# A two-layer attention kernel with experts: two expert groups per pack, the values' PSUM accumulator as two tiles, and one instruction for the experts' output rows

## The chip, the cores and the metric

The kernel runs on one core of a Trainium2 chip. The metric is the device time of one execution in microseconds, and of several executions the median. The core has a matrix engine (TensorE, PE in the profile, with its weight loads as PEld), three engines for elementwise work (VectorE or DVE, ScalarE or ACT, GpSimd or POOL), and a queue engine (SyncE or SP) that issues most of the transfers. Matrix products accumulate in PSUM; everything else works in SBUF.

## The reference, cut to what matters

There are B = 4 images of 128 channels and 64 x 64 = 4096 positions. Layer 0 is an attention between positions whose queries and keys are two 1x1 convolutions of 64 channels and whose values are a third one of 128. Layer 1 is an attention over the same positions as tokens, and then a layer of 64 experts in which each expert picks the 8 tokens of an image with the highest gate probability.

```python
x = x + conv_attn(_gn(x))                     # score softmax over j: out = einsum('nij,ncj->nci', score, asm)
t = _to_tokens(x)                             # (4, 4096, 128)
t = t + attn(_ln_t(t), Wq, Wk, Wv)
y = _ln_t(t)
probs = softmax(y @ gate_w.T + gate_b, axis=tokens)
topv, topi = top 8 tokens of every expert, of each image
pooled = sum over the 8 tokens of topv * y[topi]         # (4, 64, 128)
h   = gelu(pooled @ weight1[e, :128] + weight1[e, 128])  # 64 experts, 128 -> 512
o   = h @ weight2[e, :512] + weight2[e, 512]             # 512 -> 128
t[topi] += topv * o
return _from_tokens(t)                        # (4, 128, 64, 64)
```

For each expert there are only 4 rows (one for each image) to multiply by two weight matrices of 256 KB each: 32 MB of weights in all for little arithmetic.

## The kernel before

**Attention.** Each image's 4096 query positions are taken in NB = 8 blocks of 512 (BLK). For a block the kernel runs over all 4096 key positions: score products into PSUM (`scores`, L611), exponential by ACT (L620), then the value products, which accumulate over all key positions into one PSUM tile `av` of 128 x 2 x 512 float32, two banks. In layer 0 (`rows_products`, L545) each bank holds the sum of one half of the rows. In layer 1 (`mixed_products`, L573) the products are made with fewer multiplications from sums and differences of quarters, and the two banks hold parts that are combined afterwards. The pool `ps_av` has one buffer, so the next block's first value product must wait until the tile has been read out:

```python
avs[b, layer, n] = ps_av.tile([P, 2, BLK], F32, tag="av", name=f"av{b}_{layer}_{n}")
```

`finish_conv` (L650 to L653) reads it out after a layer 0 block: ACT copies both banks. `finish_attn` (L717 to L726) does so after a layer 1 block: bank 0 goes to `c0` (L723), bank 1 to `c1` (L724), and the two halves of bank 1, exchanged, to `sw` (L725, L726). These four copies are ACT's, but for the last block of images 0 and 1, where `copy` picks DVE for `c0` and `c1`. The very last block (`final`) divides the copies between ACT and DVE (L717 to L720). `finish_attn` goes on with the residual, the second norm and the gate products `pg` (L819 to L836), whose two halves lie in one PSUM tile of one bank; in the last block ACT reads one of the halves and DVE the other.

**Order of the work.** The order of the stages is written by hand: image and layer (0,0), (1,0), (0,1), (2,0), (1,1), (3,0), (2,1), (3,1). `stage` steps generators (the next image's norm and convolutions, routing of the image before, the finishing of the block before) between groups of key positions. Each engine works its instructions in program order; a tile framework adds the semaphore waits and reuses buffers by tag. Waits are per tile: who writes a reused buffer waits for all readers of what was in it.

**Routing.** In the stages of layer 1 and after the last block, the gate scores of an image lie in `M` as 64 experts x 4096 tokens. The eight largest of every expert are found by DVE (L881 finds and replaces them in one row of 4096), and a sum with them as weights gives `pooled`, 128 channels x (64 experts x 4 images). The last image's part is written by `last_route` (L1046), and only after that can the experts begin. `last_scores` then makes the last image's scatter weights in `M`, beside the experts (L881, L1060, L1062).

**Experts.** Sixteen groups of EG = 4 experts. For each group, step by step:

- `first_product` (L1308): one product per expert, `pooled` of 128 x 4 against 128 x 512 of weight 1, into rows 32j to 32j + 3 of one bank of `phs[0]`, a tile which `hidden_sums` (L701) had filled with zeros. DVE copies the bank to `hp` (L1313).
- `hidden`: four PE transposes of 128 x 128 (L1318), into one bank of `pht`; DVE adds the bias of weight 1 to all 512 columns (L1324), of which 16 x 4 belong to real rows and the others to the 28 padding rows of each expert; ACT applies GELU (L1328).
- `second_product` (L1338): 16 products, for each of 4 experts and 4 slices of 128 hidden units, into rows of the PSUM tile `po`. Of the 32 columns that are multiplied, 4 are real.
- every fourth group `by_expert` (L1348 to L1352) copies `po`, transposes it and puts the real rows into `outT`.

The loop runs group g of the first product, group g - 1 of `hidden` and group g - 2 of the second product in one step. The weights were packed earlier to `packed` in DRAM. Eleven places in SBUF hold groups; many are the buffers of tiles of attention that are no longer needed, and each is loaded anew for a later group (`load`, L1201) once its products have been issued.

**The end.** SP issues, in this order, the eight 256 KB reads of `first_pair` (L1379) and four 2 MB reads of `x2` (L1388), the residual, into places 0 to 3 of the weights. Each of two pairs of images then gets the experts' rows: a PE transpose (L1397), `oe` = (rows + bias of weight 2) x `inv_tot` (L1401, L1402, both DVE), products of `oe` with the scatter weights into PSUM (`px`, L1407), sixteen additions by DVE to the residual (L1414, 128 x 1024 each), and sixteen 512 KB writes of the result (L1417).

```python
oe = block_tile("c0", f"oe{i}")[:, :O]
nc.vector.tensor_add(oe, pe[:, :O], w2b)
nc.vector.tensor_scalar(oe, oe, inv_tot[:, i : i + 1], None, op0=ALU.mult)
```

Of the kernel before, what the change touches and what calls it, by code (L numbers as in the profile page):

```python
# [15 lines left out]
P = 128  # L16
# [10 lines left out]
def tile_unshifted(  # L27
# [45 lines left out]

    def sc_tile(name):
        return ps_sc.tile([P, 2, BLK], F32, tag="sc", name=name)

    def ms_tile(name):
        return ps_ms.tile([P, BLK], F32, tag="ms", name=name)
# [448 lines left out]
    def products():  # L527

        if not before:
            return  # L530
        b, layer, n, g, pts = before.pop()
        if g == 0:
            avs[b, layer, n] = ps_av.tile([P, 2, BLK], F32, tag="av", name=f"av{b}_{layer}_{n}")
        (rows_products if layer == 0 else mixed_products)(b, n, g, pts)
        if g == NG - 1:
            after.append(finish(b, layer, n))

    def rows_products(b, n, g, pts):

        for i, pt in enumerate(pts):  # L540
            for h in range(2):
                j = 2 * (2 * g + i) + h
                for r in range(2):
                    rows = bass.ts(r, CR)
                    nc.tensor.matmul(  # L545
                        avs[b, 0, n][:, r, :], lhsT=values[b, 0][rows, j, :], rhs=pt[rows, h, :],
                        start=(j == 0), stop=(j == NJ - 1),
                    )

# [14 lines left out]
    def mixed_products(b, n, g, pts):  # L564

        av = avs[b, 1, n].rearrange("p k (s t) -> p k s t", s=2)
        v, st = values[b, 1], mixed[b]  # L570

        def mm(half, bank, slot, lhsT, rhs, first, final):
            nc.tensor.matmul(  # L573
                av[bass.ts(half, HC), bank, slot, :], lhsT=lhsT, rhs=rhs, start=first, stop=final,
                skip_group_check=True,
            )

        last_g = g == NG - 1
        for i in range(2):
            j = 2 * (2 * g + i)  # L580
            mm(i, 1, 1, v[:, j, :HC], pts[i][0][:, 0, 0, :], g == 0, last_g)
        for i, (p4, tt) in enumerate(pts):
            p = 2 * g + i
            first, final = p == 0, p == NP - 1
            mm(0, 0, 1, v[:, 2 * p + 1, :HC], p4[:, 1, 0, :], first, final)
            mm(1, 1, 0, st[:, p, 0, :], tt[:, 0, :], False, final)
            mm(0, 0, 0, v[:, 2 * p, HC:], p4[:, 1, 1, :], False, final)
            mm(1, 0, 0, st[:, p, 2, :], tt[:, 1, :], first, final)
            mm(0, 1, 0, st[:, p, 1, :], p4[:, 0, 1, :], False, final)
            mm(1, 0, 1, v[:, 2 * p + 1, HC:], tt[:, 2, :], False, final)  # L590
# [54 lines left out]
    def finish_conv(b, n):  # L645
# [4 lines left out]
        nc.scalar.copy(u, av[:, 0, :])  # L650
        nc.scalar.copy(c0, av[:, 1, :])  # L651
# [43 lines left out]

    phs = []

    def hidden_sums():

        phs.append(sc_tile("ph"))  # L700
        nc.scalar.activation(  # L701
            phs[0].rearrange("p k (j c) -> p (k j) c", c=P),
            ident.unsqueeze(1).to_broadcast([P, 2 * BLK // P, P]), AF.Copy, scale=0.0,
        )

    def finish_attn(b, n):
        nm = f"{b}_1_{n}"
# [6 lines left out]
        one, two = slice(0, HB), slice(HB, BLK)  # L714
        if final:

            nc.scalar.copy(c1, av[:, 1, :])  # L717
            nc.vector.tensor_copy(c0, av[:, 0, :])
            nc.scalar.copy(sw[lo, one], av[lo, 1, one])
            nc.vector.tensor_copy(sw[hi, one], av[hi, 0, one])  # L720
        else:
            copy = nc.vector.tensor_copy if n == NB - 1 and b < B // 2 else nc.scalar.copy
            copy(c0, av[:, 0, :])  # L723
            copy(c1, av[:, 1, :])  # L724
            nc.scalar.copy(sw[lo, :], av[hi, 1, :])  # L725
            nc.scalar.copy(sw[hi, :], av[lo, 1, :])  # L726

            nc.vector.tensor_add(c1, c1, sw)
            nc.vector.tensor_add(u[:, two], c1[:, one], c1[:, two])
            nc.vector.tensor_add(u[:, two], u[:, two], c0[:, one])  # L730
            nc.vector.tensor_add(u[:, one], c1[:, two], c0[:, two])
            nc.vector.tensor_add(u[hi, one], u[hi, one], c0[hi, one])
            nc.vector.tensor_add(u[hi, one], u[hi, one], sw[hi, one])
# [82 lines left out]
                M[b // 2] = keep.tile([P, S], F32, tag="M", name=f"M{b // 2}")  # L816
            cand[b] = small.tile([P, NB, 8], F32, tag="cand", name=f"cand{b}")
        hs = slice((b % 2) * E, (b % 2 + 1) * E)
        pg = ms_tile(f"pg{b}_{n}")  # L819
        m = M[b // 2][hs, bass.ts(n, BLK)]  # L820
        for h in range(2):
            part = slice(h * E, (h + 1) * E)
            nc.tensor.matmul(
                pg[part, :HB], lhsT=gate, rhs=tg[:, bass.ts(h, HB)], start=True, stop=True
            )
        for h in range(2):
            part = slice(h * E, (h + 1) * E)
            if final and h == 1:
# [152 lines left out]
    def last_route(b, dst):  # L981
# [64 lines left out]
        nc.vector.tensor_copy(dst[:, :, b], pq[:, :E])  # L1046
        return top, neg

    def last_scores(b, top, neg):
# [231 lines left out]
    for i in range(2):  # L1281
        piece(6, 0, att_tile("sx", 4, f"w6_{i}"), 6)
    piece(6, 1, block_tile("q", "w6_2"), 6)
    mixed_place = seq.tile([P, 6 * BLK], F32, tag="mixed", name="mixed_place", bufs=1)
    piece(10, 0, mixed_place[:, : EG * H], 10)
    piece(9, 0, mixed_place[:, EG * H :], 9)
# [11 lines left out]
    scores = last_scores(B - 1, *last_top)  # L1298
    watch(1)

    pht = ps_av.tile([P, 2, BLK], F32, tag="av", name="pht")
    hps, hTs, pos = {}, {}, {}


    def first_product(g):
        ph = phs[0][:, g % 2, :]
        for j in range(EG):
            nc.tensor.matmul(  # L1308
                ph[j * PAD : j * PAD + B, :], lhsT=pooled[:, g * EG + j, :],
                rhs=weights_at(g, 0, j), start=True, stop=True,  # L1310
            )
        hps[g] = hp = block_tile("c0", f"hp{g}")
        nc.vector.tensor_copy(hp, ph)  # L1313

    def hidden(g):
        pt, hp = pht[:, g % 2, :], hps.pop(g)
        for c in range(NHC):
            nc.tensor.transpose(  # L1318
                pt[:, bass.ts(c, P)], hp.rearrange("p (q c) -> p c q", c=NHC)[:, c, :], ident
            )  # L1320
        hTs[g] = hT = block_tile("c1", f"hT{g}").rearrange(
            "p (c j b) -> p c j b", c=NHC, j=EG
        )
        nc.vector.tensor_tensor(  # L1324
            hT, pt.rearrange("p (c j b) -> p c j b", c=NHC, j=EG),
            w1bT[:, :, bass.ts(g, EG)].unsqueeze(3).to_broadcast([P, NHC, EG, PAD]), op=ALU.add,
        )
        nc.scalar.activation(hT, hT, AF.Gelu)  # L1328

    def second_product(g):  # L1330
        q, k = divmod(g, EG)
        if k == 0:
            pos[q] = ms_tile(f"po{q}").rearrange("p (g o) -> p g o", o=O)
        w2 = [weights_at(g, 1, j).rearrange("p (c o) -> p c o", c=NHC) for j in range(EG)]
        hT = hTs.pop(g)
        for c in range(NHC):
            for j in range(EG):
                nc.tensor.matmul(  # L1338
                    pos[q][bass.ts(j, PAD), k, :], lhsT=hT[:, c, j, :], rhs=w2[j][:, c, :],
                    start=(c == 0), stop=(c == NHC - 1),  # L1340
                )
        if k == EG - 1:
            by_expert(q, pos.pop(q))

    def by_expert(q, po):

# [7 lines left out]
            pt.rearrange("p (k j b) -> p k j b", k=EG, j=EG)[:, :, :, 0:B],  # L1354
        )

    for g in range(E // EG + 2):
        if g < E // EG:
            first_product(g)
        if 0 <= g - 1 < E // EG:  # L1360
            hidden(g - 1)
        if 0 <= g - 2:
            second_product(g - 2)

        for half, now, ahead in ((0, g, 11), (1, g - 2, 10)):
            if 0 <= now and now + ahead < E // EG:
                load(now + ahead, now, half)
        if g == E // EG // 2 + 2:
            next(scores)
            watch(1, phs[0][0:1, 0, 0:1])  # L1370
    next(scores)
# [23 lines left out]
    for i in range(B // 2):  # L1395
# [6 lines left out]
        nc.vector.tensor_scalar(oe, oe, inv_tot[:, i : i + 1], None, op0=ALU.mult)  # L1402
        for n in range(NB):
            px = sc_tile(f"px{i}_{n}")
            for h in range(2):
# [556 lines left out]
```

## Time and profile before

| what | value |
|---|---|
| median of 3 runs | 3240.53 us (3240.45 to 3242.14) |
| the profiled execution's own time | 3240.0 us |
| its span in the trace | 3238.3 us |
| PE busy | 3211.1 us, 99% of the span |
| DVE, ACT, POOL busy | 2152.8, 1278.7, 384.4 us |
| transfers | 222.90 MB, 69 GB/s over the span |
| attention's last value products end | about 3131 us |
| expert loop, first product to last second product | 3150.65 to 3201.86 us |
| first and last `x2` read issued | 3189.42 and 3198.60 us |
| first addition L1414 starts | 3209.09 us |
| last output write issued | 3230.35 us |

The profile is one execution. Its times count from the span's start; the execution's own time is 1.7 us above the span. A group of instructions is shown as line, engine, operation, result <- operands, and after that busy time, mean duration, and the idle time before it with who ended that. "L726" is line 726 of this kernel. In stretches of time, the DMA share is the mean busy share of the core's 16 DMA engines, so 1.0 means that all are busy throughout.

### The profile page before, as it was taken

The numbers are of one execution on the slowest core, as the hardware profiler recorded it, in microseconds if no ns is written. First come the engines' busy times: TensorE is split into PE (matmuls) and PEld (weight loads), VectorE is DVE, ScalarE is ACT, GpSimd is POOL, SyncE is SP. The second block draws the span as 40 slices with busy tenths as digits, with TensorE's granted clock in tenths as the row PEclk, the third lists the DMA queues.
The fourth block names the chain that finished last, engine by engine and source line by source line (L and its number), as shares of the span: only waits on it lengthen the run. The fifth ranks groups of instructions, "written<-read, shape, count | busy, mean of one in ns | idle before, by whom it ended". The sixth has DMA issues, their size and how long they took to land.

```text
span 3238.3 us, 49417 instructions
## 1 busy us (share of the span) xinstructions
PE 3211.1 (99%) x19630; PEld 1573.6 (49%) x19630; DVE 2152.8 (66%) x4320; ACT 1278.7 (39%) x1562; POOL 384.4 (12%) x417
## 2 busy tenths in 40 slices
PE   9999999999999999999999999999999999999997
PEld 5444444444555544444554444444444444446653
DVE  6665577556675668755775667775776566676566
ACT  3344444443433335443333334444333333343342
POOL 0111113210000003240000001332100002010001
PEclk9999999999999999999999999999999999999999
DMA  3221244223232212311120111331231111132159
GB/s 87 52 53 30 75 103 131 74 80 86 72 89 79 69 43 53 72 33 34 46 53 21 40 27 40 81 76 27 42 80 29 31 30 31 24 104 63 28 207 360
DMA packets 369120, 222.90 MB, mean 69 GB/s; under 512 B 275312, under 2 KB 300016, under 8 KB 365168
## 3 DMA queue, kind: packets, MB, share of 16 engines
q1 hardware_dynamic: 364608, 208.51, 24.1%
q10 hardware_dynamic: 3760, 10.10, 0.8%
q8 instruction: 156, 2.56, 0.3%
q0 software_dynamic: 512, 1.05, 0.1%
q14 instruction: 84, 0.69, 0.1%
HBM read 159.75 MB, written 97.19 MB: 79 GB/s over the span
## 4 chain that ended last, share of the span: by engine, by line


## 5 line engine op out<-in xcount | busy, mean ns | idle before, releaser
L620 ACT ACTIVATE pt<-ps 128x1024 f32<-128x1024 f32 x1024 | 1021.7, 1024 | 1461.0 <-PE ps L611 1396.8
L611 PE MATMUL ps<-q,t 128*64 128x512 f32 x4096 | 934.3, 592 | 0.0
L545 PE MATMUL av<-pt,asm 64*128 64x512 f32 x4096 | 922.1, 589 | 1.5 <-ACT sw L726 1.5
L635 DVE TENSOR_TENSOR sacc<-sacc,pt 128x1024 f32<-128x1024 f32 x448 | 586.1, 1308 | 291.6 <-ACT pt L620 267.8
L573 PE MATMUL av<-pt,tt 128*64 128x256 f32 x3072 | 636.2, 379 | 0.0
L545 PEld LDWEIGHTS av<-pt,asm 64*128 64x128 f32 x4096 | 396.0, 187 | 485.8 <-issue 469.3
L559 DVE TENSOR_TENSOR tt<-pt 128x512 f32<-128x512 f32 x512 | 353.9, 692 | 352.5 <-ACT pt L620 335.9
L611 PEld LDWEIGHTS ps<-q,t 128*64 128x64 f32 x4096 | 305.0, 137 | 482.5 <-issue 452.1
L573 PE MATMUL av<-tt,mixed 128*64 128x256 f32 x2048 | 525.6, 379 | 0.0
L573 PEld LDWEIGHTS av<-pt,tt 128*64 128x64 f32 x3072 | 355.9, 137 | 270.2 <-issue 135.0
L611 PE MATMUL ps<-e,e 64*128 64x512 f32 x2048 | 486.1, 592 | 0.0
L611 PEld LDWEIGHTS ps<-e,e 64*128 64x128 f32 x2048 | 196.1, 187 | 235.8 <-issue 232.2
L573 PE MATMUL av<-tt,tt 128*64 128x256 f32 x1024 | 304.6, 379 | 0.0
L573 PE MATMUL av<-pt,mixed 128*64 128x256 f32 x1024 | 304.6, 379 | 0.0
L573 PEld LDWEIGHTS av<-tt,mixed 128*64 128x64 f32 x2048 | 280.5, 137 | 9.2 <-DVE tt L559 0.2
L186 POOL TENSOR_TENSOR l_y<-l_v,mhalf 128x4 f32<-128x4 f32 x64 | 64.9, 1013 | 1634.8 <-DVE l_v L185 1634.5
L560 DVE TENSOR_TENSOR pt<-tt,pt 128x256 f32<-128x256 f32 x512 | 219.6, 429 | 16.2
L561 DVE TENSOR_TENSOR tt<-pt 128x256 f32<-128x256 f32 x512 | 219.5, 429 | 16.4
L573 PEld LDWEIGHTS av<-pt,mixed 128*64 128x64 f32 x1024 | 140.2, 137 | 65.4 <-DVE pt L560 0.3
L573 PEld LDWEIGHTS av<-tt,tt 128*64 128x64 f32 x1024 | 140.1, 137 | 4.8 <-DVE tt L561 0.3
L652 POOL TENSOR_TENSOR u<-u,c 128x512 f32<-128x512 f32 x32 | 40.9, 1277 | 557.5 <-ACT c L651 557.5
L632 DVE TENSOR_TENSOR sacc<-pt,pt 128x1024 f32<-128x1024 f32 x32 | 39.1, 1221 | 50.6 <-ACT pt L620 50.5
(298 smaller groups left out, 1797.6 us busy)
## 6 DMA issues: line engine op xcount, KB each, us to landing
wp<-in_weight_dram SPq DMA_DIRECT2D x128, 256.0 KB, 4.5
w<-wp SPq DMA_DIRECT2D x10, 1024.0 KB, 11.1
w<-wp SPq DMA_DIRECT2D x17, 512.0 KB, 10.7
xq<-in_x_dram SPq DMA_DIRECT2D x32, 256.0 KB, 3.8
rb<-inv SPq DMA_DIRECT2D x32, 256.0 KB, 3.4
xT<-xt SPq DMA_DIRECT2D x128, 64.0 KB, 2.2
ak<-xT SPq DMA_DIRECT2D x32, 256.0 KB, 3.7
t<-kt SPq DMA_DIRECT2D x128, 64.0 KB, 2.2
```

What stands on the lines that cost most here:

```text
L186: nc.gpsimd.tensor_tensor(y[:, :k], v[:, :k], mhalf[:, :k], op=ALU.pow)
L545: nc.tensor.matmul(avs[b, 0, n][:, r, :], lhsT=values[b, 0][rows, j, :], rhs=pt[rows, h, :], start=(j == 0), stop=(j == NJ - 1),)
L559: nc.vector.tensor_sub(tt[:, 0:2, :], p4[:, :, 1, :], p4[:, 0, :, :])
L560: nc.vector.tensor_add(p4[:, 0, 1, :], tt[:, 1, :], p4[:, 0, 0, :])
L561: nc.vector.tensor_sub(tt[:, 2, :], p4[:, 1, 0, :], p4[:, 0, 1, :])
L573: nc.tensor.matmul(av[bass.ts(half, HC), bank, slot, :], lhsT=lhsT, rhs=rhs, start=first, stop=final, skip_group_check=True,)
L611: nc.tensor.matmul(ps[part, h, :], lhsT=key[:, part], rhs=q[rows, :], start=True, stop=True,)
L620: nc.scalar.activation(pt, ps, AF.Exp, scale=scale)
L632: nc.vector.tensor_add(sums[b, n], pts[0], pts[1])
L635: nc.vector.tensor_add(sums[b, n], sums[b, n], pt)
L652: nc.gpsimd.tensor_add(u, u, c0)
```

## The change

There are five edits.

1. `av` becomes two tiles of one bank each (`av_tiles`). At the last block of images 0 and 1 only `c0` stays with DVE; `c1` goes to ACT like the two `sw` copies.
2. In the last block the gate products `pg` go into two PSUM tiles, one for each half.
3. Two groups of experts make a pack (PK = 2). `pooledP` is a copy of `pooled` with 8 columns per expert for each of the two groups: group k of the pack has its 4 rows in columns 4k to 4k + 3, and zeros in the other four. The two groups' first products accumulate in the same bank, 8 rows per expert, so that one copy `hp` and four transposes serve both. The bias of weight 1 is added to the 64 real columns of each slice alone, once per group, which also packs them densely; one GELU of 128 columns serves both groups, and the second product multiplies 4 columns. `hidden` is one tile, of which one half serves even packs and the other odd packs.
4. The tiles `po` are two fixed ones, zeroed once by ACT (`zeros_into`), since the second products no longer write the padding rows. `outT` moves into `pooled`'s place, and the reloads of places follow the packs.
5. The product of the bias of weight 2 with `inv_tot` is made ahead of the loop (`biases`), and `oe` comes from PSUM by one SCALAR_TENSOR_TENSOR.

```diff
+    def av_tiles(name):
+        return [ps_av.tile([P, BLK], F32, tag=f"av{k}", name=f"av{k}_{name}") for k in range(2)]
...
-            avs[b, layer, n] = ps_av.tile([P, 2, BLK], F32, tag="av", name=f"av{b}_{layer}_{n}")
+            avs[b, layer, n] = av_tiles(f"{b}_{layer}_{n}")
...
             copy = nc.vector.tensor_copy if n == NB - 1 and b < B // 2 else nc.scalar.copy
-            copy(c0, av[:, 0, :])
-            copy(c1, av[:, 1, :])
-            nc.scalar.copy(sw[lo, :], av[hi, 1, :])
-            nc.scalar.copy(sw[hi, :], av[lo, 1, :])
+            copy(c0, av[0])
+            nc.scalar.copy(c1, av[1])
+            nc.scalar.copy(sw[lo, :], av[1][hi, :])
+            nc.scalar.copy(sw[hi, :], av[1][lo, :])
...
-        pg = ms_tile(f"pg{b}_{n}")
+        pgs = [ms_tile(f"pg{b}_{n}_{h}") for h in range(2 if final else 1)]
...
+    PK = 2
+    pooledP = block_tile("tb", "pooledP").rearrange("p (e m) -> p e m", e=E)
...
+    nc.gpsimd.memset(pooledP, 0.0)
+    for k in range(PK):
+        nc.gpsimd.tensor_copy(
+            by_pack[0][:, :, k, :, k * B : k * B + B - 1], by_pack[1][:, :, k, :, 0 : B - 1]
+        )
...
-    last_top = last_route(B - 1, pooled)
-    outT = block_tile("tb", "outT")[:, : B * E].rearrange("p (b e) -> p b e", e=E)
+
+    def last_pooled(pq):
+        by = pq.rearrange("p (g k j) -> p g k j", k=PK, j=EG)
+        for k in range(PK):
+            nc.vector.tensor_copy(by_pack[0][:, :, k, :, k * B + B - 1], by[:, :, k, :])
+
+    last_top = last_route(B - 1, last_pooled)
+    outT = pooled.rearrange("p e b -> p (e b)").rearrange("p (b e) -> p b e", e=E)
...
+    phts = av_tiles("pht")
+    pos = [ms_tile(f"po{i}").rearrange("p (g o) -> p g o", o=O) for i in range(2)]
+    for po in pos:
+        zeros_into(po)
+    hidden_place = block_tile("c1", "hidden")
+    biases = [hidden_place[:, BLK // 2 + i * O :][:, :O] for i in range(B // 2)]
+    for i, bias in enumerate(biases):
+        nc.vector.tensor_scalar(bias, w2b, inv_tot[:, i : i + 1], None, op0=ALU.mult)
...
     def first_product(g):
-        ph = phs[0][:, g % 2, :]
+        k, pk = g % PK, g // PK
+        ph = phs[0][:, pk % 2, :]
         for j in range(EG):
             nc.tensor.matmul(
-                ph[j * PAD : j * PAD + B, :], lhsT=pooled[:, g * EG + j, :],
-                rhs=weights_at(g, 0, j), start=True, stop=True,
-            )
-        hps[g] = hp = block_tile("c0", f"hp{g}")
-        nc.vector.tensor_copy(hp, ph)
+                ph[j * PAD : j * PAD + PK * B, :], lhsT=pooledP[:, g * EG + j, :],
+                rhs=weights_at(g, 0, j), start=(k == 0), stop=(k == PK - 1),
+            )
+        if k == PK - 1:
+            hps[pk] = hp = block_tile("c0", f"hp{pk}")
+            nc.vector.tensor_copy(hp, ph)
...
-        nc.vector.tensor_tensor(
-            hT, pt.rearrange("p (c j b) -> p c j b", c=NHC, j=EG),
-            w1bT[:, :, bass.ts(g, EG)].unsqueeze(3).to_broadcast([P, NHC, EG, PAD]), op=ALU.add,
-        )
-        nc.scalar.activation(hT, hT, AF.Gelu)
+        at = hidden_place[:, bass.ts(pk % 2, PK * NHC * EG * B)]
+        hT = at.rearrange("p (k c j b) -> p k c j b", k=PK, c=NHC, j=EG)
...
+        for k in range(PK):
+            g = pk * PK + k
+            nc.vector.tensor_tensor(
+                hT[:, k], p4[:, :, :, bass.ts(k, B)],
+                w1bT[:, :, bass.ts(g, EG)].unsqueeze(3).to_broadcast([P, NHC, EG, B]),
+                op=ALU.add,
+            )
+            hTs[g] = hT[:, k]
+        nc.scalar.activation(at, at, AF.Gelu)
...
-                    pos[q][bass.ts(j, PAD), k, :], lhsT=hT[:, c, j, :], rhs=w2[j][:, c, :],
+                    po[j * PAD : j * PAD + B, k, :], lhsT=hT[:, c, j, :], rhs=w2[j][:, c, :],
...
+    packs = E // EG // PK
+    for pk in range(packs + 1):
+        mine = range(pk * PK, pk * PK + PK) if pk < packs else ()
+        for g in mine:
             first_product(g)
+            reload(g, 11, 0)
+            if g == mine[0] and pk > 0:
+                hidden(pk - 1)
+        if pk == packs:
+            hidden(pk - 1)
+        if pk > 0:
+            for g in range((pk - 1) * PK, pk * PK):
+                second_product(g)
+                reload(g, 10, 1)
+        if pk == packs // 2:
             next(scores)
             watch(1, phs[0][0:1, 0, 0:1])
...
-        nc.vector.tensor_add(oe, pe[:, :O], w2b)
-        nc.vector.tensor_scalar(oe, oe, inv_tot[:, i : i + 1], None, op0=ALU.mult)
+        nc.vector.scalar_tensor_tensor(
+            oe, in0=pe[:, :O], scalar=inv_tot[:, i : i + 1], in1=biases[i], op0=ALU.mult,
+            op1=ALU.add,
+        )
```

More of the change, by code (lines that the diff above doesn't have):

```diff
@@ L545, in rows_products @@
                     nc.tensor.matmul(
-                        avs[b, 0, n][:, r, :], lhsT=values[b, 0][rows, j, :], rhs=pt[rows, h, :],
+                        avs[b, 0, n][r], lhsT=values[b, 0][rows, j, :], rhs=pt[rows, h, :],
                         start=(j == 0), stop=(j == NJ - 1),
@@ L564, in mixed_products @@
     def mixed_products(b, n, g, pts):
-        av = avs[b, 1, n].rearrange("p k (s t) -> p k s t", s=2)
+        av = [t.rearrange("p (s t) -> p s t", s=2) for t in avs[b, 1, n]]
         v, st = values[b, 1], mixed[b]
@@ L573, in mm @@
             nc.tensor.matmul(
-                av[bass.ts(half, HC), bank, slot, :], lhsT=lhsT, rhs=rhs, start=first, stop=final,
+                av[bank][bass.ts(half, HC), slot, :], lhsT=lhsT, rhs=rhs, start=first, stop=final,
                 skip_group_check=True,
@@ L649, in finish_conv @@
         s2 = sums.pop((b, n))
-        nc.scalar.copy(u, av[:, 0, :])
-        nc.scalar.copy(c0, av[:, 1, :])
+        nc.scalar.copy(u, av[0])
+        nc.scalar.copy(c0, av[1])
         nc.gpsimd.tensor_add(u, u, c0)
@@ L696, in tile_unshifted, with zeros_into @@
     phs = []
+    def zeros_into(t):
+        nc.scalar.activation(
+            t, ident.unsqueeze(1).to_broadcast([P, t.shape[1], P]), AF.Copy, scale=0.0
+        )
     def hidden_sums():
         phs.append(sc_tile("ph"))
-        nc.scalar.activation(
-            phs[0].rearrange("p k (j c) -> p (k j) c", c=P),
-            ident.unsqueeze(1).to_broadcast([P, 2 * BLK // P, P]), AF.Copy, scale=0.0,
-        )
+        zeros_into(phs[0].rearrange("p k (j c) -> p (k j) c", c=P))
     def finish_attn(b, n):
@@ L715, in finish_attn @@
         if final:
[L717 to L720, printed above, removed]
+            nc.scalar.copy(c1, av[1])
+            nc.vector.tensor_copy(c0, av[0])
+            nc.scalar.copy(sw[lo, one], av[1][lo, one])
+            nc.vector.tensor_copy(sw[hi, one], av[0][hi, one])
         else:
             copy = nc.vector.tensor_copy if n == NB - 1 and b < B // 2 else nc.scalar.copy
[L723 to L726, printed above, removed]
+            copy(c0, av[0])
+            nc.scalar.copy(c1, av[1])
+            nc.scalar.copy(sw[lo, :], av[1][hi, :])
+            nc.scalar.copy(sw[hi, :], av[1][lo, :])
             nc.vector.tensor_add(c1, c1, sw)
@@ L823, in finish_attn @@
             nc.tensor.matmul(
-                pg[part, :HB], lhsT=gate, rhs=tg[:, bass.ts(h, HB)], start=True, stop=True
+                pgs[-h][part, :HB], lhsT=gate, rhs=tg[:, bass.ts(h, HB)], start=True, stop=True
             )
@@ L827, in finish_attn @@
             part = slice(h * E, (h + 1) * E)
+            pg = pgs[-h]
             if final and h == 1:
@@ L1045, in last_route @@
         nc.tensor.matmul(pq[:, :E], lhsT=halves, rhs=twin, start=False, stop=True)
-        nc.vector.tensor_copy(dst[:, :, b], pq[:, :E])
+        dst(pq[:, :E])
         return top, neg
@@ L1283, in tile_unshifted @@
     piece(6, 1, block_tile("q", "w6_2"), 6)
+    PK = 2
+    pooledP = block_tile("tb", "pooledP").rearrange("p (e m) -> p e m", e=E)
+    by_pack = [
+        t.rearrange("p (g k j) m -> p g k j m", k=PK, j=EG) for t in (pooledP, pooled)
+    ]
+    nc.gpsimd.memset(pooledP, 0.0)
[3 more added lines that the diff above has]
+        )
     mixed_place = seq.tile([P, 6 * BLK], F32, tag="mixed", name="mixed_place", bufs=1)
@@ L1299, in tile_unshifted, with hidden @@
     watch(1)
-    pht = ps_av.tile([P, 2, BLK], F32, tag="av", name="pht")
-    hps, hTs, pos = {}, {}, {}
+    phts = av_tiles("pht")
[3 more added lines that the diff above has]
+    hidden_place = block_tile("c1", "hidden")
+    hps, hTs = {}, {}
+    biases = [hidden_place[:, BLK // 2 + i * O :][:, :O] for i in range(B // 2)]
+    for i, bias in enumerate(biases):
+        nc.vector.tensor_scalar(bias, w2b, inv_tot[:, i : i + 1], None, op0=ALU.mult)
     def first_product(g):
-        ph = phs[0][:, g % 2, :]
+        k, pk = g % PK, g // PK
+        ph = phs[0][:, pk % 2, :]
         for j in range(EG):
             nc.tensor.matmul(
-                ph[j * PAD : j * PAD + B, :], lhsT=pooled[:, g * EG + j, :],
-                rhs=weights_at(g, 0, j), start=True, stop=True,
-            )
-        hps[g] = hp = block_tile("c0", f"hp{g}")
-        nc.vector.tensor_copy(hp, ph)
-    def hidden(g):
-        pt, hp = pht[:, g % 2, :], hps.pop(g)
+                ph[j * PAD : j * PAD + PK * B, :], lhsT=pooledP[:, g * EG + j, :],
+                rhs=weights_at(g, 0, j), start=(k == 0), stop=(k == PK - 1),
+            )
+        if k == PK - 1:
+            hps[pk] = hp = block_tile("c0", f"hp{pk}")
+            nc.vector.tensor_copy(hp, ph)
+    def hidden(pk):
+        pt, hp = phts[pk % 2], hps.pop(pk)
         for c in range(NHC):
@@ L1320, in hidden @@
             )
-        hTs[g] = hT = block_tile("c1", f"hT{g}").rearrange(
-            "p (c j b) -> p c j b", c=NHC, j=EG
-        )
-        nc.vector.tensor_tensor(
-            hT, pt.rearrange("p (c j b) -> p c j b", c=NHC, j=EG),
-            w1bT[:, :, bass.ts(g, EG)].unsqueeze(3).to_broadcast([P, NHC, EG, PAD]), op=ALU.add,
-        )
-        nc.scalar.activation(hT, hT, AF.Gelu)
+        at = hidden_place[:, bass.ts(pk % 2, PK * NHC * EG * B)]
+        hT = at.rearrange("p (k c j b) -> p k c j b", k=PK, c=NHC, j=EG)
+        p4 = pt.rearrange("p (c j m) -> p c j m", c=NHC, j=EG)
+        for k in range(PK):
[7 more added lines that the diff above has]
+        nc.scalar.activation(at, at, AF.Gelu)
     def second_product(g):
         q, k = divmod(g, EG)
-        if k == 0:
-            pos[q] = ms_tile(f"po{q}").rearrange("p (g o) -> p g o", o=O)
+        po = pos[q % 2]
         w2 = [weights_at(g, 1, j).rearrange("p (c o) -> p c o", c=NHC) for j in range(EG)]
@@ L1342, in second_product @@
         if k == EG - 1:
-            by_expert(q, pos.pop(q))
+            by_expert(q, po)
     def by_expert(q, po):
@@ L1355, in by_expert, with reload @@
         )
-    for g in range(E // EG + 2):
-        if g < E // EG:
-            first_product(g)
[L1360 to L1368, printed above, removed]
+    def reload(g, ahead, half):
+        if g + ahead < E // EG:
+            load(g + ahead, g, half)
+    packs = E // EG // PK
+    for pk in range(packs + 1):
+        mine = range(pk * PK, pk * PK + PK) if pk < packs else ()
+        for g in mine:
+            first_product(g)
+            reload(g, 11, 0)
[8 more added lines that the diff above has]
+        if pk == packs // 2:
             next(scores)
```

## The prediction

> **What bounds the kernel now.** I read the page first, then the transfer shares by stretch, then the timeline of single stretches, then the waits. The page says where the bulk is:
>
> ```profile
> PE 3211.1 (99%) x19630; PEld 1573.6 (49%) x19630; DVE 2152.8 (66%) x4320; ACT 1278.7 (39%) x1562; POOL 384.4 (12%) x417
> DMA  3221244223232212311120111331231111132159
> ```
>
> PE is busy for 99%, so up to the last attention block (it ends near 3131 us) only PE time counts, and only what makes PE wait can be won. The DMA row ends in 5 and 9: in the last 160 us the transfers are a second candidate. The same row by stretch of the end (columns: window, its length, busy us of PE, PEld, DVE, ACT, POOL, granted clock, DMA share, GB/s):
>
> ```profile
> 3130.00:3186.00 56.00, 51.31 (x620) 33.59 (x616) 34.21 (x87) 13.19 (x23) 1.05 (x1) 1.00 1.02 408
> 3186.00:3191.00 5.00, 4.37 (x64) 2.40 (x68) 3.35 (x5) 1.26 (x2) 0.00 (x0) 1.00 0.42 134
> 3191.00:3210.00 19.00, 14.57 (x206) 8.23 (x198) 12.02 (x15) 11.77 (x13) 5.65 (x3) 0.90 1.00 415
> 3210.00:3213.00 3.00, 3.00 (x8) 1.09 (x8) 2.04 (x3) 0.44 (x1) 3.00 (x2) 0.51 0.42 173
> 3216.00:3234.00 18.00, 11.35 (x42) 3.01 (x40) 13.14 (x12) 0.00 (x0) 0.00 (x0) 0.98 1.01 398
> ```
>
> From 3130 on the transfers are the bound: a share of 1.0 at 400 to 415 GB/s, with two holes. The first (3186 to 3191) lies between the last expert weights with the `first_pair` reads and the four 2 MB `x2` reads (L1388). The second (3210 to 3213, and a third of 3215 to 3216) lies between those reads and the output writes (L1417). Who makes the holes is in the timeline (start us, us, engine, line, operation; in brackets the idle time before and who ended it):
>
> ```profile
> 3160.30 1.04 PE L1308 MATMUL ph<-w,pooled 128*4 128x512 f32 x8
> 3161.27 0.75 PE L1318 MATMUL pht<-ident,hp 128*128 128x128 f32 x4
> 3161.95 1.08 PE L1338 MATMUL po<-w,hT 128*32 128x128 f32 x32
> 3162.84 1.04 PE L1308 MATMUL ph<-w,pooled 128*4 128x512 f32 x8
> 3186.63 1.04 PE L1308 MATMUL ph<-tt,pooled 128*4 128x512 f32 x8 [2.58 <-DVE hp L1313]
> 3189.42 0.37 SPq L1388 DMA_DIRECT2D t<-x  x1
> 3204.46 4.71 DVE L1402 TENSOR_SCALAR oe<-oe,inv_tot 128x128 f32<-128x128 f32 x2
> 3209.09 1.21 DVE L1414 TENSOR_TENSOR t<-t,px 128x1024 f32<-128x1024 f32 x1
> ```
>
> An expert group costs PE 2.54 us (0.97 first products, 0.68 transposes, 0.89 second products, no gap). The `x2` read at 3189.42 goes into the buffer that groups 10 and 11 used; in SP's waits L1388 waits 12.1 us in all for `po` of L1338. So hole one is the expert loop being late. Hole two is the final additions being late: DVE starts them at 3209.09, after two multiplications of `oe` that took 4.71 us, where the same form at L900 took 0.29. One more place, in the attention part, at a change of batch:
>
> ```profile
> 1158.95 0.69 DVE L723 COPY c<-av 128x512 f32<-128x512 f32 x1 [0.79 <-PE av L573]
> 1159.56 0.68 DVE L724 COPY c<-av 128x512 f32<-128x512 f32 x1
> 1160.33 0.58 ACT L725 COPY sw<-av 64x512 f32<-64x512 f32 x1 [3.42 <-DVE c L724]
> 1160.92 0.58 ACT L726 COPY sw<-av 64x512 f32<-64x512 f32 x1
> 1161.55 3.70 PE L545 MATMUL av<-pt,asm 64*128 64x512 f32 x16 [0.76 <-ACT sw L726]
> ```
>
> Four copies empty the one `av` tile one after the other, ACT behind DVE, and PE waits 0.76 us for the last. The same stands at 1939.19, again 0.76; these two make up the 1.5 us of idle time that the page puts down at L545 to L726; its other large groups of PE matmuls show none.
>
> **What the Trainium skill says.** "PSUM — Partial Sum Buffer", section "PSUM bank collisions raise a hardware error": two engines must not touch one bank at once, two readers included; different banks may be used together. The trace orders even more: at 3131.78 ACT copies one bank of `av`, and DVE's copy of the other bank starts at 3132.40, when ACT's has ended. So the tile is what is ordered, and two tiles should free both. "SBUF — State Buffer", section "Who interferes with whom": DVE's two-port modes, into which `tensor_scalar` can go, share a port pair with GpSimd under an exclusive lock, while a DVE instruction with one SBUF input outside those modes doesn't contend. The trace agrees: L1402 takes 2.4 us each beside POOL's L1062 (2.42 us each, from 3204.35), and L1414 with one PSUM input stays at 1.22 beside it. "DMA: Bandwidth & Descriptors", Specifications, has a fabric ceiling of 435 GB/s; the trace's best stretches, 408 to 415 GB/s at a full share, leave little above.
>
> **The change, part by part.**
> 1. *`av` as two tiles; the second copy at the two batch ends goes from DVE to ACT.* ACT now copies bank 1 (0.59) and the two `sw` halves (0.58 each) from 1158.95 on, done near 1160.73; DVE's bank 0 is done at 1159.64. PE asks for bank 0 at 1160.79. Both stalls go: **2 x 0.76 = -1.52 us**. What is queued behind on ACT, the exponentials of 1161.52, starts 0.8 earlier, although ACT has one copy more. PE is the limit there, so all of it arrives at the end of attention, and every weight load that waits for it moves along.
> 2. *Last block: copies in parallel, `pg` in two tiles.* DVE's `M` add at 3142.50 waited for ACT's 0.47 us; now it doesn't. With the copies some 0.5 to 0.7 us of this chain; the filler products until 3147.74 let through about 0.5. The transfers are full beside it: 0 at the end.
> 3. *Two groups per pack.* First products stay 16 x 0.85: 592 ns per matmul stands for 4 columns (L1308) and for 64 (L611), so 8 cost the same. Transposes: 8 x 0.68 instead of 16 x 0.68, -5.4. Second products with 4 columns instead of 32: the nearest row is the old one, 0.89; bounds 0 and -0.1 per group. Copies `hp` on DVE: 8 x 0.69 instead of 16; bias additions 16 of 64 elements, 0.22 to 0.27 each by the 128x64 copy (L1352, 0.27), for 16 x 0.69; ACT 8 activations of about 0.31 for 16 x 0.63. Waits: the first products of pack 1 wait for the copy of pack 0, and so do those of pack 2 for pack 1 (1.0 us each, as 0.81 at 3152.50 shows for two halves of `ph`); after that the copy hides behind two second products (1.78). The 4.42 us MATCH_REPLACE8 (L881) still stalls PE for about 2.1 (2.58 now). Adding PE's list up from the start of the experts, the loop takes some 42.5 us instead of 51.2 (3150.65 to 3201.86), and group 10's second products end near 3181.7 in the changed run's time (3189.36 now).
> 4. *Added:* a POOL memset and two copies for `pooledP` (a few us near 3122, POOL idle there until 3137); DVE's two bias multiplications (0.29 each, behind the products' latency); two ACT zeroings of `po` (0.6 each, between 3148 and 3150, while ACT waits for the first `hT`); one more small DVE copy ahead of the first product (0.15). Cover: transfers run at full share through all of it. Were it gone, about 0.3 us.
> 5. *`oe` as one SCALAR_TENSOR_TENSOR from PSUM.* 0.35 us by the same form at L763, for 0.5 + 4.71. With 3, the first addition starts near 3196 instead of 3209.09.
>
> What 3 and 5 bring at the end isn't their sum. `x2` reads issued by 3184 close hole one; additions 13 us earlier close hole two. In bytes: hole one 5 x (1 - 134/415) = 3.4 us, with the slow restart 3.8; hole two 3 x (1 - 173/400) = 1.7, and 0.36 at 3215. Together **-5.5 to -5.9**. The sixteen additions (16 x 1.22 = 19.5) end near 3219, long before the last write: DVE has 7 us to spare. After the holes are closed the next to be late is the transfer itself.
>
> Sum: -1.5 - 5.7 = -7.2 on the profiled execution's 3240.0 us (span 3238.3, 1.7 around it) gives 3232.8; the median of the runs is 0.5 above it, so **3233.3**.
>
> **Rivals.**
> - *Both holes close (the forecast).* 3231.5 to 3235.0. For it: full shares on both sides of each hole. Chance 0.62.
> - *A hole stays*, because reads and writes at once move less, or because the loads' buffers come free in pairs: -1.5 and only 2.1 of the rest, 3236.9. Against: the 256 KB write of L780, issued at 3137.76 beside the weight loads, left the total at 395 to 420 GB/s from 3141 to 3144. Chance 0.22. If the two stalls of 0.76 also stay, since something else ends them, 1.5 more.
> - *PE and DVE set the end after all:* 8.7 and 4.4 us arrive, 3226. Against: the 56 us at a share of 1.02. Chance 0.08.
> - *Slower:* a pack runs as one serial chain. `hidden` is a single tile for both halves and the biases, and the trace shows tiles ordered as a whole. Then PE stands for copy 0.97, transposes 0.75, additions 0.5, activation 0.31, hand-overs 0.35: 2.9 us per pack, six packs ahead of group 10: 3199 instead of 3181.7, and the `x2` reads are 9.5 us later than now: 3240 + 9.5 - 2.1 = 3247. It starts to cost at 0.5 us per pack, and turns the result slower above 2.6. Against: PE's order has each transpose behind the second products of the pack before, so the tile is free by then. Chance 0.08.
>
> **Numbers.** 3233.3 us; range 3230.0 to 3237.0: the forecast's own, the open hole, and the edge towards the third case. A change under 0.2% (6.5 us) can't be told from none. Faster by more: most of the first case and the third, 0.62; within it: the second and the rest of the first, 0.31; slower 0.07.
>
> **What would show it.** PE without a gap at L545's successor; a DMA share of 1.0 from 3130 through the last write, no hole over 1 us; first `x2` issue near 3184 and first addition near 3196; `oe` in 0.35 us; transposes 32. Wrong if a hole stays with the loop faster, if PE waits over 0.5 us per pack, or if the GB/s drop where reads and writes mix.

## The result, and the profile after

The changed kernel takes **3232.71 us** (median of 10 executions, 3232.03 to 3233.59); the kernel before, beside it on the same chip, 3241.69 (3240.0 to 3244.1). The ratio is 0.9972 with a 95% interval of 0.9962 to 0.9982, which is 5.8 to 12.3 us less. The two profiled executions took 3240.0 and 3232.45 us, with spans of 3238.3 and 3230.6: 7.6 and 7.7 us less, where the forecast's sum was 7.2. The medians differ by more, 9.0: the profiled execution of the kernel before is the fastest of its ten.

From the page of the changed kernel, the rows that answer to those of before; the last number of the matmul row is the idle time ahead of it:

```profile
PE 3202.3 (99%) x19598; PEld 1574.2 (49%) x19598; DVE 2134.0 (66%) x4311; ACT 1272.0 (39%) x1558; POOL 387.5 (12%) x420
DMA  3121235223232212311221111231131111122149
L548 PE MATMUL av<-pt,asm 64*128 64x512 f32 x4096 | 922.4, 590 | 0.0
```

PE has 32 instructions fewer (the transposes) and 8.8 us less to do, and the value products of L548 (L545 before) have no idle time ahead of them, where 1.5 us stood. From the start of the first exponential of attention to that of the last the trace of before has 3101.15 us (24.56 to 3125.71) and this one 3099.41 (24.41 to 3123.82): 1.74 less, about 0.83 of it at each of the two batch ends. What stands there now, at the first of them:

```profile
1158.75 0.58 ACT L728 COPY c<-av 128x512 f32<-128x512 f32 x1 [2.00 <-PE av L576]
1158.79 0.69 DVE L727 COPY c<-av 128x512 f32<-128x512 f32 x1 [0.79 <-PE av L576]
1159.35 0.58 ACT L729 COPY sw<-av 64x512 f32<-64x512 f32 x1
1159.94 0.58 ACT L730 COPY sw<-av 64x512 f32<-64x512 f32 x1
1160.47 3.80 PE L548 MATMUL av<-pt,asm 64*128 64x512 f32 x16
```

DVE and ACT start within 0.04 us of each other, and PE's L548 has no bracket: it doesn't wait, where L545 waited 0.76 us in the kernel before.

The end of the kernel by stretch (window, length, busy us of PE, PEld, DVE, ACT, POOL, granted clock, DMA share, GB/s):

```profile
3128.00:3148.00 20.00, 18.96 (x152) 16.14 (x148) 12.47 (x54) 6.09 (x13) 1.05 (x1) 1.00 1.02 412
3148.00:3153.00 5.00, 4.10 (x36) 1.17 (x36) 2.26 (x12) 1.93 (x3) 0.00 (x0) 1.00 0.99 332
3153.00:3183.00 30.00, 26.98 (x498) 15.18 (x494) 12.40 (x23) 1.81 (x6) 0.00 (x0) 1.00 1.02 413
3183.00:3187.00 4.00, 4.00 (x36) 1.39 (x25) 1.32 (x4) 0.01 (x1) 0.00 (x0) 1.00 1.08 403
3187.00:3208.00 21.00, 17.51 (x180) 7.95 (x178) 12.38 (x16) 10.29 (x11) 9.44 (x4) 0.92 1.01 419
3208.00:3225.00 17.00, 7.71 (x28) 1.91 (x26) 9.41 (x8) 0.00 (x0) 0.00 (x0) 0.84 1.03 416
```

Both holes are gone: where 134 GB/s (3186 to 3191) and 173 GB/s (3210 to 3213) stood, the share is 1.0 through the reads, the stretch where reads and writes mix, and the writes. One shallow dip has come up, 332 GB/s at 3148 to 3153: 5 x (413 - 332) is 0.4 MB, or 1.0 us of transfers. It will matter below. A pack in the timeline, and the start of the final additions:

```profile
3167.02 1.04 PE L1336 MATMUL ph<-w,pooledP 128*8 128x512 f32 x8
3167.99 0.75 PE L1347 MATMUL av_pht<-ident,hp 128*128 128x128 f32 x4
3168.84 0.35 DVE L1355 TENSOR_TENSOR hidden<-av_pht,w1bT 128x64 f32<-128x64 f32 x2 [2.78 <-PE av_pht L1347]
3169.31 0.31 ACT L1361 ACTIVATE hidden<-hidden 128x128 f32<-128x128 f32 x1 [4.10 <-DVE hidden L1355]
3169.68 1.93 PE L1370 MATMUL po<-w,hidden 128*4 128x128 f32 x64
3195.03 0.61 DVE L1440 SCALAR_TENSOR_TENSOR oe<-poe,inv_tot,hidden 128x128 f32<-128x128 f32 x2 [0.42 <-PE poe L1436]
3197.51 1.22 DVE L1455 TENSOR_TENSOR t<-t,px 128x1024 f32<-128x1024 f32 x1 [1.87 <-PE px L1448]
```

Two groups share one set of transposes and one activation of 0.31 us; PE fills the 0.9 us between its transposes and its second products with the next first products. The two `oe` take 0.61 us together instead of 0.5 + 4.71, and the first addition starts at 3197.51 instead of 3209.09.

### The profile page after: what moved, and what is told of

It reads as the page before. It is cut to its first block, busy times and chain, and to the rows that moved or that the text cites. A ratio compares the mean times of both kernels' runs of the same rounds, so it can differ in the third digit from the quotient of the medians.

```text
span 3230.6 us, 49325 instructions
## 1 busy us (share of the span) xinstructions
PE 3202.3 (99%) x19598; PEld 1574.2 (49%) x19598; DVE 2134.0 (66%) x4311; ACT 1272.0 (39%) x1558; POOL 387.5 (12%) x420
## 3 DMA queue, kind: packets, MB, share of 16 engines
q8 instruction: 156, 2.56, 0.3%
## 4 chain that ended last, share of the span: by engine, by line
PE 98%; DVE 1%; issue 1%; DMA 0%; POOL 0%; SPq 0%; ACT 0%; POOLq 0%; ACTq 0%; DVEq 0%
PE ps L614 41%; PE av L548 27%; PE av L576 24%; PE pq L517 1%; PE pv L759 1%; PE pe L372 1%; PE ph L1336 0%; PE pa L374 0%; PE pa L351 0%; PE pe L319 0%; PE pg L827 0%; PE po L1370 0%; PE px L1448 0%; DVE w L1455 0%; DMA first_x<-in_x_dram 0%
## 5 line engine op out<-in xcount | busy, mean ns | idle before, releaser
L548 PE MATMUL av<-pt,asm 64*128 64x512 f32 x4096 | 922.4, 590 | 0.0
L548 PEld LDWEIGHTS av<-pt,asm 64*128 64x128 f32 x4096 | 401.6, 187 | 478.5 <-issue 477.2
```

Of the source, the lines that this page charges most:

```text
L548: nc.tensor.matmul(avs[b, 0, n][r], lhsT=values[b, 0][rows, j, :], rhs=pt[rows, h, :], start=(j == 0), stop=(j == NJ - 1),)
```

## The experiments

Theory A is the forecast's: from 3128 on the transfers set the end. Theory B, its third rival: PE and DVE do. Where a number stands "against the changed kernel", its median of 3232.71 above and of 3232.26 in the run below is the base. The changed kernel wasn't run again beside the later ones; the kernel before was, with medians of 3241.27 to 3241.69, so the bases carry over to within some 0.5 us, and differences under about 1 us are not told from none.

**The changed kernel again (r1_after).** 

> The changed kernel again, as the base for the other kernels of this row. Both theories: 3232 to 3234 us, 7 to 9 us below the kernel before.

 Measured: 3232.26 us beside 3241.27 for the kernel before.

**`oe` by two instructions again (r2_no_oe).**

```diff
-        nc.vector.scalar_tensor_tensor(oe, in0=pe[:, :O], ...
+        nc.vector.tensor_add(oe, pe[:, :O], w2b)
+        nc.vector.tensor_scalar(oe, oe, inv_tot[:, i : i + 1], None, op0=ALU.mult)
```

> The changed kernel, with oe made again by two instructions (add, then tensor_scalar). The two tensor_scalars fall beside POOL's subtractions and take about 2.4 us each, so the first addition starts about 4.6 us later, near 3202 instead of 3197.5. Theory A (the transfers set the end): the x2 reads keep the transfers busy until 3209, and the first writes can be issued near 3205, so hole two stays closed: 0 to +0.5 us against the changed kernel. Theory B (the chain of PE and DVE sets the end): +4.6 us.

 Measured: 3231.84 us, -0.4 to -0.9 against the changed kernel. In its timeline of DVE, `oe` is slow again beside POOL:

```profile
3195.04 0.49 DVE L1440 TENSOR_TENSOR oe<-poe,w2b 128x128 f32<-128x128 f32 x2 [0.42 <-PE poe L1436]
3195.45 3.87 DVE L1441 TENSOR_SCALAR oe<-oe,inv_tot 128x128 f32<-128x128 f32 x2
3199.24 2.34 DVE L1453 TENSOR_TENSOR t<-t,px 128x1024 f32<-128x1024 f32 x2
```

The first addition is 1.7 us later (4.6 were expected) and the last write is issued 2.8 us later (3220.81 for 3217.96), and the end doesn't move. So DVE's chain does not set it, and in the changed kernel the fifth edit is worth nothing.

**Only `av` in two tiles, with the `c1` copy on ACT (r5_av).** The edit to the kernel before is the first of the change. 

> The kernel before with only av as two tiles and the c1 copy of two batch ends on ACT. Expected: both stalls of 0.76 us gone, the last value products 1.5 to 1.9 us earlier, both holes as before: -1.5 to -1.9 us. Rival: other work takes PE's place or the stalls move to another wait, 0.

 Measured: 3239.12 us, -2.2, ratio 0.9993 (0.9985 to 1.0002): by the interval alone not told from no change, but the trace has attention 1.75 us shorter.

**The two halves of that edit (r6_split, r7_move).**

```diff
r6_split: two tiles, but
-            nc.scalar.copy(c1, av[1])
+            copy(c1, av[1])
r7_move: one tile, but
-            copy(c1, av[:, 1, :])
+            nc.scalar.copy(c1, av[:, 1, :])
```

Each ran once, at 3239.3 and 3242.3 us; what counts is the two stalls in the trace.

> The kernel before with av as two tiles, but c0 and c1 both copied by DVE at the two batch ends. Bank 0 is free 0.7 us after PE's last product; bank 1 waits for DVE's second copy and ACT's two, as before. Expected: each stall stays at 0.6 to 0.8 us, now at the first product into bank 1. Rival (the split alone frees PE): no gap.

 Missed: PE has no gap there, and attention is 1.48 us shorter. The timeline of r6_split:

```profile
1159.43 0.69 DVE L727 COPY c<-av 128x512 f32<-128x512 f32 x1 [0.74 <-PE av L576]
1160.04 0.68 DVE L726 COPY c<-av 128x512 f32<-128x512 f32 x1
1160.16 0.58 ACT L728 COPY sw<-av 64x512 f32<-64x512 f32 x1 [2.73 <-DVE c L727]
1161.15 3.92 PE L548 MATMUL av<-pt,asm 64*128 64x512 f32 x16
```

The order had turned as well: DVE copies bank 1 first (L727), and ACT's copies of bank 1 run beside DVE's copy of bank 0. 

> The kernel before with one av tile, but the c1 copy at the two batch ends on ACT. If a tile is what is ordered, ACT's copies wait for DVE's copy of the other bank: 0.69 + 0.58 + 0.58 + 0.58 instead of 0.69 + 0.68 + 0.58 + 0.58, and each stall is 0.6 to 0.7 us. If only the bank is ordered, ACT and DVE go side by side and the stalls are gone.

 Measured: each stall 0.70, and attention is 0.11 us shorter. The timeline of r7_move:

```profile
1158.78 0.69 DVE L723 COPY c<-av 128x512 f32<-128x512 f32 x1 [0.79 <-PE av L573]
1159.50 0.59 ACT L724 COPY c<-av 128x512 f32<-128x512 f32 x1 [2.77 <-DVE c L723]
1161.33 3.70 PE L545 MATMUL av<-pt,asm 64*128 64x512 f32 x16 [0.70 <-ACT sw L726]
```

ACT's copy of bank 1 starts when DVE's copy of bank 0 has ended: with one tile the tile is ordered, not the bank. So the split brings the gain, in r6_split with the order that came with it, and the move alone 2 x 0.06 us.

**`av` and `oe`, but no packs (r4_av_oe).** The first and fifth edits on the kernel before. 

> The kernel before with av in two tiles (and the c1 copy on ACT) and oe by one instruction, but the expert groups one by one as before. Theory A: hole one stays (the loop is as late as before), hole two closes: about -1.9 for av and -2.4 for hole two, -4.3 us against the kernel before. Theory B: -1.9 and the 4.6 us that oe gets shorter, -6.5.

 Measured: 3237.16 us, -4.1, ratio 0.9987 (0.9981 to 0.9994): theory A's number. By stretch:

```profile
3128.00:3183.00 55.00, 51.74 (x626) 33.87 (x622) 33.38 (x87) 13.08 (x23) 1.04 (x1) 1.00 1.02 410
3184.00:3189.00 5.00, 4.05 (x47) 2.27 (x50) 2.94 (x6) 1.26 (x2) 0.00 (x0) 0.66 0.38 135
3209.00:3211.00 2.00, 1.82 (x8) 0.60 (x8) 1.90 (x3) 1.24 (x2) 2.00 (x1) 1.00 0.99 356
```

Hole one stays; hole two is all but closed (356 GB/s). Hole one isn't quite that of before, though: the second line has a granted clock of 0.66, where the kernel before has 1.00 in its hole. After the stall beside the replacement the clock fell to 0.5 from 3185.3 to 3188.8, so that PE freed the place of the first `x2` read late:

```profile
3184.95 1.52 PE L1315 MATMUL ph<-tt,pooled 128*4 128x512 f32 x8 [2.58 <-DVE hp L1320]
3189.24 0.37 SPq L1395 DMA_DIRECT2D t<-x  x1
```

The read goes out 4.3 us after the end of the stall, for 2.8 in the kernel before (3186.63 and 3189.42). Over 8 us around the hole this kernel moves 145 GB/s (3184 to 3192), the kernel before 220 (3185 to 3193): at 410 GB/s that is 5.2 us lost, for 3.7. r5_av has the same drop of the clock (157 GB/s in 3184 to 3192).

With the packs in its place, r2_no_oe has both holes closed. Against r5_av the `oe` edit alone brings -2.0, the packs alone (r2_no_oe) -7.3, and both -6.4 to -6.9: the packs close both holes, and `oe` only the second.

**`pg` in one tile again (r8_no_pg).** 

> The changed kernel, with pg of the last block in one tile again. DVE's M addition waits for ACT's read, about 0.5 us on the chain to the experts' start. Theory A (transfers set the end): 0 against the changed kernel. Theory B: up to +0.5.

 Measured: 3232.74 us, 0 to +0.5. Its M addition waits again for ACT (1.24 us idle ahead of it, 0.74 in the changed kernel), and the end doesn't show it. Little of it gets as far as the experts: from attention's last value product to the first expert product it takes 18.83 us (3128.14 to 3146.97), for 18.66 in the changed kernel (3129.43 to 3148.09). Between the gate products and the routing's next PE work stand 50 filler products (5.85 us) in both.

**1.5 MB of weights loaded earlier (r3_early).**

```diff
+            for i, first in ((0, NG // 2), (1, NG // 2 + 1)):
+                if first <= g < first + EG - 1:
+                    load_piece(i, 1, pieces[i, 1][g - first])
...
-                load(0, 0, 1)
+                load_piece(0, 1, pieces[0, 1][EG - 1])
-    load(1, 1, 1)
+    load_piece(1, 1, pieces[1, 1][EG - 1])
```

> The changed kernel, with second-half weights of groups 0 and 1 loaded in pieces of one expert (256 KB): three of four pieces each are issued during the last attention block, as soon as the quarter of the keys or values that they overwrite has been used, instead of at the block's end. So 1.5 MB leave the stretch that is full of transfers for one in which the DMA share is 0.35. Theory A: 1.5 MB at 410 GB/s are 3.8 us; about 0.7 us of it lost again in a hole ahead of the first x2 read, whose place PE frees at 3182.4: -3.0 us against the changed kernel. Theory B: 0, since no instruction of PE or DVE is touched and no weight was waited for.

 Missed: 3233.79 us, 1.1 to 1.5 **more** than the changed kernel. Theory A can't be right as it stands, so two kernels asked where a megabyte counts.

**One megabyte less early, or moved early with few pieces (r9_less_first, r11_early2).** The first leaves out `load(1, 1, 1)`, and group 1's second products use what is in the place. The second:

```diff
+            for i, first in ((0, NG // 2), (1, NG // 2 + 1)):
+                if first <= g < first + 2:
+                    part_of_second(i, g - first, 1)
...
-                load(0, 0, 1)
+                part_of_second(0, 2, 2)
-    load(1, 1, 1)
+    part_of_second(1, 2, 2)
```

> The changed kernel without one 1 MB weight load (second half of group 1), which is issued at the end of attention and lands near 3140; group 1's second products read what was in the place, so part of the result is not the reference's. Theory A as I had it (bytes anywhere in the full stretch count): 1 MB at 410 GB/s, -2.5 us against the changed kernel. Theory A2 (after r3): from about 3148 on the transfers go on only with what places the experts' first products release, and PE's chain sets when that is; a megabyte ahead of 3148 only makes the backlog end sooner, and a hole opens at 3149 to 3152: 0 to -1.2 us. Theory B (PE and DVE to the end): 0.

 Measured: 3232.81 us, +0.1 to +0.6. 

> The changed kernel with 1 MB of the second halves of groups 0 and 1 (two pieces of 256 KB each) loaded during the last block, and the reloads of these places in one piece of 1 MB as in the changed kernel. Theory A: -2.5 us against the changed kernel. Theory A2: the hole at 3149 to 3152 takes what was gained, 0 to -1.2 us. If r3 lost its time to its many small pieces alone, this one shows -2 or more.

 Measured: 3232.98 us, +0.3 to +0.7. A megabyte ahead of 3148 is worth nothing that these runs can show, left out or moved. By stretch, first r1_after, then r9_less_first:

```profile
3140.00:3147.00 7.00, 6.54 (x57) 6.22 (x57) 6.03 (x23) 2.60 (x8) 0.00 (x0) 1.00 1.03 420
3147.00:3149.00 2.00, 1.65 (x18) 1.21 (x21) 0.87 (x6) 0.81 (x2) 0.00 (x0) 1.00 0.98 387
3149.00:3153.00 4.00, 3.19 (x32) 0.90 (x24) 1.35 (x7) 1.42 (x2) 0.00 (x0) 1.00 1.06 367
```

```profile
3140.00:3147.00 7.00, 6.54 (x59) 6.28 (x59) 5.63 (x23) 2.87 (x7) 0.00 (x0) 1.00 1.02 411
3147.00:3149.00 2.00, 1.65 (x17) 0.76 (x20) 1.38 (x10) 1.02 (x2) 0.00 (x0) 1.00 0.36 111
3149.00:3153.00 4.00, 3.19 (x28) 0.80 (x20) 1.11 (x4) 1.13 (x2) 0.00 (x0) 1.00 0.90 263
```

The megabyte comes back as a hole: 2 x (387 - 111) + 4 x (367 - 263) is 0.97 MB. What the next loads wait for stands in the waits of SP's queue, here of the changed kernel from 3140 to 3190 (us in total, times, longest):

```profile
SPq L1427 <- PE po L1370: 5.0, 3, 4.2
SPq L1206 <- PE pool L1050: 4.4, 1, 4.4
SPq L1206 <- PE ph L1336: 2.9, 3, 1.4
```

One load waits 4.4 us until `last_route` (L1050) leaves its buffer, and what is queued behind it waits along; the next ones wait for the experts' first products (L1336). They go out at 3147.55 and 3149.53. In r9_less_first the first of them waits longer, 5.3 us, and still goes out 0.20 us after L1050 starts, as in the changed kernel (3147.13 and 3147.33 here, 3147.35 and 3147.55 there): with fewer bytes ahead of it, it still goes when PE lets it. So ahead of 3148 it is PE's chain again that counts.

r3_early has the same hole, 277 and 216 GB/s. That it came out slower than the changed kernel has a second part: from 3128 to 3147 it moves 386 GB/s, for r1_after's 412, at the same share of 1.02. It had gained 1.1 MB by 3128; 0.5 MB goes there and 0.8 MB in the hole (236 GB/s for 374 from 3147 to 3153), and small losses later make it more than was gained. Why the rate is lower isn't shown.

**One megabyte less late (r10_less_last).** The loop over `first_pair` reads starts at block 4. 

> The changed kernel without four of the eight first_pair reads (1 MB, landing near 3183 to 3185); four of the sixteen scatter products then use other data, so part of the result is not the reference's. Theories A and A2: the x2 reads are issued in time (3182.9, bytes from about 3185, when the queue would run dry), -2.5 us against the changed kernel. Theory B: 0.

 Missed in the median: 3231.78 us, -0.5 to -0.9. But none of the six executions lies near it: three took 3230.42 to 3230.60, which is 1.7 to 2.3 under the bases and close to theory A's 2.5, and three 3232.96 to 3233.47, which is no gain. The only trace is of one of the slower three (3232.96), and what follows is shown for it alone. By stretch:

```profile
3179.00:3183.00 4.00, 3.71 (x20) 1.03 (x24) 0.59 (x3) 0.31 (x1) 0.00 (x0) 0.57 1.02 391
3183.00:3187.00 4.00, 4.00 (x77) 2.21 (x76) 1.64 (x3) 0.00 (x0) 0.00 (x0) 1.00 0.52 151
```

The transfers run dry at 3183, and the first `x2` read was issued at 3184.42 (3182.95 in the changed kernel). It waited for the place that second products release, as SP's waits of this kernel show:

```profile
SPq L1427 <- PE po L1370: 5.2, 1, 5.2
```

Against r1_after's 398 GB/s in 3183 to 3187 the hole costs 4 x (398 - 151), 0.99 MB: here all of it. In this execution PE was late, too: the granted clock was 0.57 from 3179 to 3183, as its timeline shows (the first line's eight products took 1.04 us elsewhere):

```profile
3179.29 1.66 PE L1336 MATMUL ph<-tt,pooledP 128*8 128x512 f32 x8 [2.04 <-DVE hp L1342]
3180.87 1.13 PE L1347 MATMUL av_pht<-ident,hp 128*128 128x128 f32 x4
3183.30 0.94 PE L1370 MATMUL po<-t,hidden 128*4 128x128 f32 x28
```

From the end of the stall to these second products, which free the place, it took 4.01 us, for 2.66 in the changed kernel (3178.70 to 3181.36): 1.35 us of the 1.5 by which the read was late. That the faster three executions kept the full clock would fit, but no trace shows it.

**A later second half of the loop (r12_twice).** `tc.keep_in_program_order(replace(b, top, z))` stands twice. 

> The changed kernel with the 4.42 us MATCH_REPLACE8 in the expert loop issued twice (the second gives the same result), so that the second half of the loop is 4.4 us later. Theories A and A2: the first x2 read moves from 3182.9 to about 3187.3 and its bytes to 3189, the queue before it runs dry at 3187.4: a hole of about 1.8 us, +1.8 us against the changed kernel. Theory B: +4.4 us.

 Measured: 3233.84 us, +1.1 to +1.6. PE stood still for 2.56 us more, not 4.4, since two groups of products were ready beside the second replacement; the first `x2` read went out at 3185.08, 2.1 later, and the hole (286 GB/s from 3183 to 3187, against 398) is 1.1 us. The chain of PE and DVE was really later by 3.0 to 3.3 us at the first addition (3200.80, for 3197.85 in r1_after and 3197.51 in the changed kernel), two to three times what arrives at the end: theory B is ruled out here, even with the smaller delay. By this run the slack of the `x2` reads is about 1 us.

## Why the prediction was right, and where not

- **The sum:** 3233.3 forecast, 3232.71 measured. This is closer than its parts deserve: the forecast took 7.2 from a base of 3240.5, and in the later runs the medians moved by 9.0, from 3241.69. Between the profiled executions the change was 7.6.
- **Stalls of `av`:** -1.52 forecast, -1.74 in the trace. The edit's reason held (the tile is ordered), but not its division: r6_split shows that the copy need not have moved.
- **Holes:** -5.5 to -5.9 forecast for both. With 1.74 for the stalls, the 7.6 between the profiled executions leave 5.9. For hole one alone the forecast had 3.4 to 3.8, and the trace of before loses 3.7 there. r4_av_oe, with hole one open, stands 4.4 to 4.9 us above the changed kernel, and lies on the rival "a hole stays" (3236.9 for 3237.16); its hole is longer than that of before because of the clock (5.2 us), which the forecast didn't have. What makes the medians move by more than the profiled executions stays open.
- **Hole two:** 1.7 + 0.36 forecast; r4_av_oe against r5_av gives 2.0. But the credit was shared out wrongly: the step that gives part 5 a share fails, since r2_no_oe shows that the packs close hole two without it. The forecast had said that the parts don't add up.
- **The loop:** 42.5 us forecast, 44.7 measured (3148.09 to 3192.83; 51.2 before). Both early waits are there, 0.81 us each where 1.0 was put, and the replacement's stall is 2.04 for 2.1. Left out of the list was a wait of 0.94 us ahead of the last second products. Too small was the price of the first products, 0.85 a group: that holds from one group of them to the next, but ahead of the transposes it is 0.97 (3167.02 to 3167.99 above, and 0.97 in the forecast's own line of before). The longer loop cost nothing: the first `x2` read went out at 3182.95 for 3184.
- **`pg`:** 0 at the end, as forecast. But the forecast let about 0.5 us of it through to the experts and had full transfers cover it; by r8_no_pg it is 0.17. **`oe`:** 0.30 us each for 0.35.
- **What had been read too simply:** "from 3130 on the transfers are the bound". A DMA share of 1.0 said so, and it was true for what the change touches. But r9_less_first shows a gate near 3148, and r12_twice and the traced execution of r10_less_last one near 3183: a point where the next transfers wait for a place that PE releases. At the first the transfers come early, by 0.5 to 1.0 us (the dip in r1_after and in the changed kernel), so saved bytes ahead of it give nothing. At the second the release comes early, by about 1 us in r12_twice; the faster executions of r10_less_last speak for more. After it the transfers are the bound: r2_no_oe, r4_av_oe and r12_twice move with the holes and not with DVE. That they are so between the two gates is argued from the full share; no run took bytes away there alone.
- **Slower, by a serial pack:** no sign of it; PE's waits in the packs sum to 3.7 us for `hp`, and none is per pack. This rival's limit for "slower" (2.6 us per pack) doesn't follow from its own numbers: by these, 2.9 us in each of six packs make the result 7.4 us slower than before, so that it breaks even near 1.7.

No version faster than the changed kernel came out of this. By this account a faster one would have to move both gates (PE's chain from 3130 to 3148, and the stall of 2.04 us beside the replacement) and then save bytes. That was not tried.

## What to carry to other kernels

Cost a hole in the transfers by its missing bytes, and ask for each edit which hole it closes: two edits that close the same one don't add up. A full DMA share does not prove that a saved byte counts: ahead of a gate, where the queue waits for a buffer, a saved megabyte can come back as a hole, so look for the release that the next transfer waits for. Compare the granted clock before you compare two holes, and look at the single executions before you trust a median. Where two engines read out two banks of one PSUM tile, two tiles let them run side by side.

## What was not expected of the hardware

After a stall in the expert loop the clock that is granted to PE fell to half for about 3.5 us in some of the profiled executions. After the stall of 2.04 us beside the replacement it fell in r3_early and r10_less_last (from 3179), and not in the changed kernel, r1_after, r2_no_oe, r8_no_pg, r9_less_first, r11_early2 and r12_twice. After a stall of 2.56 to 2.58 us it fell in r4_av_oe, r5_av, r6_split and r12_twice, and not in the kernel before and r7_move. In r10_less_last it made the first `x2` read about 1.4 us late, more than the slack that r12_twice shows at that gate. What decides it stays open, and so does how many of the executions without a trace had it.
